# A recurrent layer on one core: hidden-state products of half B from bf16 parts, its two gates in one PSUM bank, x products without combinations

## The chip, the cores and the metric

The kernel runs on one NeuronCore of one Trainium2 chip. The metric is the device time of one execution in microseconds. A core has TensorE (PE, matrix products into PSUM), VectorE (DVE), ScalarE (ACT), GpSimd (POOL) and SyncE (SP, which issues DMAs here). They run at the same time, each its own instructions in order, and wait for each other through semaphores. In the profile's rows PEld is TensorE's weight load, the loading of the operand that stays in the array while the other one streams past it.

## The reference

A gated recurrent layer over 512 time steps, batch 8, 512 inputs, 512 hidden units; all float32. Cut to what matters:

```python
def step(h, x_t):
    fused = sigmoid(concat([x_t, h]) @ w_W + w_b)      # 1024 x 1024
    hidden_state, output_state = split(fused, 2)       # r and z
    memory_state = x_t @ wx_W + wx_b + hidden_state * (h @ wh_W + wh_b)
    h_new = output_state * h + (1.0 - output_state) * tanh(memory_state)
    return h_new, h_new
out = x + scan(step, h0, x)
```

Below, r and z are the two sigmoids and hh is `h @ wh_W + wh_b`. Each step needs the h of the step before, so the 512 steps follow one another; only the products with x can be done ahead.

## The kernel before, in words

**Layout.** The 512 hidden units are cut into four chunks k of 128, and the 128 partitions hold the units of a chunk in four strips of 32. A product takes a chunk of h (128 x 32: 8 batch columns for each of four steps of a group, so that the step's rows fall where its place in the group wants them; the other columns hold zeros) as the operand that stays, streams weights past it, and writes 32 PSUM partitions, one strip j. Four strips, four products side by side.

**Halves and banks.** The units are also cut into two halves: A (chunks 0 and 1) and B (chunks 2 and 3). Bank A (192 columns) gathers hh, z and r of half A, bank B (128 columns) r and hh of half B, bank C (64 columns) z of half B. A step runs its products in the order of `ORDER`: "A0 B0 A1 A2 A3 B1 B2 B3 C0 C1 C2 C3", letter and chunk of h. A0, B0 and A1 need only the new h of half A, A2 that of half B too. Behind them a step takes seven x products (`take(later, 7)`).

**The x side.** Four steps are a group; banks are kept twice, for even and odd groups. The x products of two groups are formed together with seven instead of eight half products (`products`), from sums of weights (`weight_sum`, DVE, in steps 1 to 8) and sums of x (`x_sum`, POOL), collected in the two banks `xps` and put together by DVE and ACT (the `o, u` branches). `spread` copies them into the banks A, B and C, `turn_x` turns the x part of the memory state into its place.

**A step after its products.** DVE turns r, hh and z of a half from PSUM to SBUF (32 x 32 block transposes), ACT takes the sigmoids (r into `md0`, 1-z into `hd0`). `memory` is a scan over (0, hh, r, x) tuples that gives r*hh+x for one chunk of 8 batch columns, then tanh on ACT; `update` is a scan that gives the new h of a chunk. DVE's order is: r, h, z and the two memories of half A, r and h of half B, first update of A, z of B, second update of A, memories and updates of B. POOL adds x and h into the output tile after the updates of B, first half B, then half A. `idle` memsets of one element on DVE stand behind the z transpose and at the step's end.

**Names.** `tr`, `tz`: turned gates; `md0`, `md1`, `hd0`: operands of the scans; `m`: memory state; `hTA`, `hTB`: the states, eight buffers each; `ot`: output tile; `xin`, `head`: x.

All engines' orders are the order of the code (`manual_schedule`). SP loads x in chunks of 16 steps and stores the output likewise; all weights are loaded once, at the start.

Of the kernel before, what the change touches and what calls it, by code (L numbers as in the profile page):

```python
# [7 lines left out]
F32 = mybir.dt.float32  # L8
# [13 lines left out]
DVE_FILL = 23  # L22
IDLE = 3
# [9 lines left out]
HALF = 192  # L33

AL, BE = (0, slice(64, 256)), (0, slice(256, 448))
GA, DE = (1, slice(64, 256)), (1, slice(256, 448))

XP = {"A": slice(0, 192), "X": slice(192, 320), "C": slice(320, 384), "B": slice(384, 512)}
# [3 lines left out]
def tile_cond_rnn_residual(  # L42
# [5 lines left out]
    wa_d: bass.AP,  # L48
    wb_d: bass.AP,
    wb3_d: bass.AP,  # L50
# [83 lines left out]
    def wh(bank, k, j):  # L134
        return wa[:, k, j] if bank == "A" else wb[:, k, j, {"C": slice(0, 64), "B": slice(64, 192)}[bank]]
# [3 lines left out]
    def pair(n, name, rows, slots):  # L139

        return const.tile([P, 2, rows, slots], F32, name=name).rearrange("p c n s -> p n c s")

    NH = 2 * GS
    hT = [[pair(n, f"hT{n}{i}", 32, 3) for i in range(NH)] for n in "AB"]

    md0 = [[pair(n, f"md0{n}{i}", 32, 2) for i in range(2)] for n in "AB"]
    md1 = [[pair(n, f"md1{n}{i}", 32, 2) for i in range(2)] for n in "AB"]
    hd0 = [[pair(n, f"hd0{n}{i}", B, 3) for i in range(2)] for n in "AB"]  # L150
# [7 lines left out]
    for j in range(NQ):  # L158
        nc.vector.memset(ones[32 * j : 32 * j + 1, j], 1.0)

    nc.scalar.activation(const.tile([P, 1], F32, name="table"), zeros[:, :1], AF.Sigmoid)
    for n, t_ in enumerate(hd0[0] + hd0[1] + md0[0] + md0[1] + hT[0] + hT[1]):
# [3 lines left out]
    idle = const.tile([P, IDLE], F32, name="idle")  # L166

    tw = [const.tile([P, 2, NQ, HALF], F32, name=f"tw{n}") for n in range(4)]
    sx = [[const.tile([P, 2, GS * B], F32, name=f"sx{n}{q}") for q in range(2)] for n in range(4)]
    step_bias = const.tile([P, HALF], F32, name="stepbias")  # L170
    even = const.tile([P, 256], F32, name="even")
    odd = [const.tile([P, 256], F32, name=f"odd{q}") for q in range(2)]
    both = const.tile([P, HALF], F32, name="both")

    def state(hf, i, slot=2):

        s = i % GS
        return hT[hf][i % NH][:, B * s : B * s + B, :, slot]

    ctx.enter_context(tc.manual_schedule())  # L180
    banks = [
        {n: psum.tile([P, w], F32, name=f"{n}{q}") for n, w in BANKS.items()}
        for q in range(2)
    ]
    xps = [psum.tile([P, 512], F32, name=f"xp{q}") for q in range(2)]
# [17 lines left out]
    nc.vector.tensor_copy(bias, xps[0])  # L203
    for hf in range(2):
        for slot in (0, 2):
            nc.vector.tensor_copy(
                state(hf, 0, slot), hin[:, 2 * hf : 2 * hf + 2].rearrange("p c b -> p b c")
            )
# [13 lines left out]
    def seed(g):  # L222

        nc.scalar.copy(xps[g % 2], bias)  # L224

    def prefill(g):

        c, t0 = divmod(g * GS, TC)
        for k in range(NQ):
            for j in range(NQ):  # L230
                mm(
                    xps[g % 2][32 * j : 32 * j + 32, 64:448],
                    x_of(c, k, t0, GS),
                    wx[:, k, j, :],
                )
            yield

    def late(g):

        if g == 0:  # L240
            return xps[0][:, 256:512]
        return even if g % 2 == 0 else odd[g // 2 % 2]

    def part(g, c0, c1):

        return late(g)[:, c0 - 256 : c1 - 256] if c0 >= 256 else xps[g % 2][:, c0:c1]

    def spread(g, names):

        for n in names:  # L250
            nc.scalar.copy(banks[g % 2][n], part(g, XP[n].start, XP[n].stop))

    def turn_x(g, e):

        c0 = XP["X"].start + 32 * e
        nc.vector.transpose(md1[e // 2][g % 2][:, :, e % 2, 1], part(g, c0, c0 + 32))

    def reg(r):
        return xps[r[0]][:, r[1]]

    def wx_of(kh, ch):
        return wx[:, 2 * kh : 2 * kh + 2, :, HALF * ch : HALF * ch + HALF]

    def x_half(o, n, kh):

        return x_of(o // 2, slice(2 * kh, 2 * kh + 2), 8 * (o % 2) + GS * n, GS)

    def weight_sum(n, k=slice(0, 2), j=None):

        a, b = [  # L270
            (wx_of(0, 1), wx_of(0, 0)),
            (wx_of(1, 1), tw[0]),
            (wx_of(1, 1), wx_of(0, 1)),
            (wx_of(1, 0), tw[1]),
        ][n]
        at = (slice(0, P), k, slice(0, NQ) if j is None else slice(2 * j, 2 * j + 2))
        nc.vector.tensor_tensor(tw[n][at], a[at], b[at], ALU.subtract)

    def x_sum(o, n):

        t_ = [q[o % 2] for q in sx]
        a, b, op = [
            (x_half(o, 1, 0), x_half(o, 1, 1), ALU.add),
            (t_[0], x_half(o, 0, 0), ALU.subtract),
            (x_half(o, 0, 0), x_half(o, 1, 0), ALU.subtract),
            (x_half(o, 0, 1), t_[1], ALU.subtract),
        ][n]
        nc.gpsimd.tensor_tensor(t_[n], a, b, op)

    def products(o):  # L290

        t_ = [q[o % 2] for q in sx]
        for to, lhs, rhs in (
            (AL, x_half(o, 0, 0), wx_of(0, 0)),
            (DE, t_[0], tw[0]),
            (BE, t_[1], tw[1]),
            (AL, x_half(o, 0, 1), wx_of(1, 0)),
            (GA, t_[2], tw[2]),
            (BE, t_[3], wx_of(1, 1)),
            (GA, x_half(o, 1, 1), tw[3]),  # L300
        ):
            for k in range(2):
                for j in range(NQ):
                    mm(reg(to)[32 * j : 32 * j + 32], lhs[:, k], rhs[:, k, j])
                    yield
# [7 lines left out]
    def x_side():  # L313
        for o in range(2, NG // 2):
            yield from products(o)

# [3 lines left out]
    later = x_side()  # L320
    first = {g: prefill(g) for g in (1, 2, 3)}
    weight_sum(0)
    weight_sum(2)
    spread(0, "BCA")
    for e in range(NQ):
        turn_x(0, e)

    pool_done = {}
    for i in range(T):
        g, s = divmod(i, GS)  # L330
        c, t = divmod(i, TC)
        ps = banks[g % 2]
# [5 lines left out]
        for n in (ORDER if i else FIRST).split():  # L338
            if n == "x":
                take(first[1], 1)  # L340
                continue
            bank, k = n[0], int(n[1])
            hs = hT[k // 2][i % NH][:, :, k % 2, 2]
            for j in range(NQ):
                j = (j + turn[0]) % NQ
                to = ps[bank] if i or bank != "A" else xps[0][:, XP["A"]]
                mm(to[32 * j : 32 * j + 32, :], hs, wh(bank, k, j))
        if i < 5:
# [87 lines left out]
        if i == 0:  # L436

            seed(2)
# [167 lines left out]
```

## Time and profile before

| what | value |
|---|---|
| time, median of 3 runs | 1670.06 us (1669.73 to 1671.35) |
| profiled execution, span | 1670.8 us |
| PE busy | 1659.0 us, 99% |
| DVE busy | 1090.5 us, 65% |
| ACT busy | 1029.9 us, 62% |
| POOL busy | 301.9 us, 18% |
| DMA, share of 16 engines | q1 4.0%, instructions 1.8% |
| granted TensorE clock, mean | 0.999 |

The profiled execution's own time is its span: the first to the last instruction. A row of a group shows line, engine, operation, what it writes `<-` what it reads, partitions x elements and type, how often, then its busy time in us, the mean ns of one, and the idle time of the engine before it with what ended that. A row of a timeline begins with start and length in us; neighbouring instructions of a kind are merged (`x16`), and the length is that of the whole group. The ends of matmuls are modelled and they are pipelined, so how fast products follow each other is read from start to start. Every matmul of the program is line 188, a helper's; the tile tells which it is.

### The profile page before, as it was taken

The page shows a single profiled execution, that of the slowest core. Times are in us where ns is not written, and L with a number is a line of the kernel's source. Part 1 is how long each engine was busy: PE and PEld are TensorE (multiplying, and loading weights), DVE is VectorE, ACT ScalarE, POOL GpSimd, SP SyncE. Part 2 cuts the span into 40 slices and gives each one's busy share as a digit, 9 for nine tenths or more (in the row PEclk, how much of TensorE's full clock was granted, in tenths as well). Part 3 has the DMA queues.
Part 4 walks back from the last instruction along what each step waited for, and adds up shares of the span by engine and source line. Part 5 has one row for each costly group of instructions (what it writes and reads, how often), then busy time and mean ns, then how long its engine had stood idle before and what let it go on. Part 6 is the DMA issues. An engine that isn't in the chain of part 4 may idle for free.

```text
span 1670.8 us, 129875 instructions
## 1 busy us (share of the span) xinstructions
PE 1659.0 (99%) x56238; PEld 1637.5 (98%) x56238; DVE 1090.5 (65%) x9387; ACT 1029.9 (62%) x5822; POOL 301.9 (18%) x1281
## 2 busy tenths in 40 slices
PE   8999999999999999999999999999999999999998
PEld 5999999999999999999999999999999999999997
DVE  6666666666666666666666666666666666666666
ACT  3666666666666666666666666666666666666665
POOL 1111111111111111111111111111111111111111
PEclk9999999999999999999999999999999999999999
DMA  4000000000000000000000000000000000000000
GB/s 179 17 5 17 18 18 17 17 6 17 17 18 18 5 17 18 17 17 5 18 17 17 18 11 12 18 17 17 18 5 17 17 18 17 5 17 12 11 12 10
DMA packets 11525, 31.40 MB, mean 19 GB/s; under 512 B 1220, under 2 KB 1732, under 8 KB 10824
## 3 DMA queue, kind: packets, MB, share of 16 engines
q1 hardware_dynamic: 10800, 22.94, 4.0%
q8 instruction: 440, 7.21, 1.8%
q14 instruction: 133, 1.09, 0.2%
q10 hardware_dynamic: 152, 0.16, 0.0%
HBM read 14.70 MB, written 8.39 MB: 14 GB/s over the span
## 4 chain that ended last, share of the span: by engine, by line
PE 98%; DVE 1%; DMA 0%; issue 0%; ACT 0%
PE A L188 44%; PE B L188 23%; PE xp L188 20%; PE C L188 12%; DMA rows<-in_bias_dram 0%; DVE tr L374 0%; DVE m L358 0%; DVE tz L374 0%; DVE md1B L390 0%; DVE md1A L390 0%; DVE hTA L358 0%; DVE bias L203 0%; ACT hTB L216 0%; ACT xp L224 0%; DVE rows L120 0%
## 5 line engine op out<-in xcount | busy, mean ns | idle before, releaser
L188 PE MATMUL A<-wa,hTA 128*32 128x192 f32 x8176 | 638.2, 329 | 2.3 <-DVE hTA L358 2.3
L188 PE MATMUL B<-wb,hTA 128*32 128x128 f32 x8192 | 573.8, 273 | 0.0
L188 PE MATMUL A<-wa,hTB 128*32 128x192 f32 x8176 | 507.4, 326 | 0.5 <-DVE hTB L358 0.5
L188 PEld LDWEIGHTS B<-wb,hTA 128*32 128x32 f32 x8192 | 471.2, 122 | 1.4 <-issue 0.2
L374 DVE STREAM_TRANSPOSE tr<-A 128x64 f32<-128x64 f32 x511 | 127.7, 250 | 463.5 <-PE A L188 463.5
L188 PE MATMUL B<-wb,hTB 128*32 128x128 f32 x8192 | 398.9, 273 | 0.0
L188 PEld LDWEIGHTS A<-wa,hTA 128*32 128x32 f32 x8176 | 385.4, 123 | 7.6 <-DVE hTA L358 4.0
L188 PEld LDWEIGHTS A<-wa,hTB 128*32 128x32 f32 x8176 | 372.9, 122 | 2.7 <-DVE hTB L358 0.8
L216 ACT ACTIVATE md0A<-tr 128x16 f32<-128x16 f32 x512 | 112.3, 219 | 421.0 <-DVE tr L374 421.0
L507 POOL TENSOR_TENSOR ot<-xin,hTB 128x16 f32<-128x16 f32 x503 | 125.9, 250 | 1324.5 <-DVE hTB L358 1314.0
L188 PEld LDWEIGHTS B<-wb,hTB 128*32 128x32 f32 x8192 | 321.5, 122 | 0.1
L188 PE MATMUL C<-wb,hTA 128*32 128x64 f32 x8192 | 289.4, 219 | 0.0
L188 PE MATMUL C<-wb,hTB 128*32 128x64 f32 x8192 | 288.9, 220 | 0.2 <-issue 0.2
L188 PEld LDWEIGHTS C<-wb,hTA 128*32 128x32 f32 x8192 | 266.7, 122 | 0.0
L188 PE MATMUL xp<-tw,sx 128*32 128x192 f32 x2976 | 237.2, 326 | 0.1
L188 PEld LDWEIGHTS C<-wb,hTB 128*32 128x32 f32 x8192 | 229.2, 123 | 0.4 <-issue 0.4
L358 DVE TENSOR_TENSOR_SCAN hTB<-hd0B,hTB 128x24 f32<-128x24 f32 x1024 | 157.8, 195 | 101.0 <-ACT hTB L216 99.8
L358 DVE TENSOR_TENSOR_SCAN hTA<-hd0A,hTA 128x24 f32<-128x24 f32 x1024 | 191.0, 187 | 0.0
L188 PE MATMUL xp<-wx,xin 128*32 128x192 f32 (+1 forms) x2048 | 182.4, 331 | 0.7 <-issue 0.5
L216 ACT ACTIVATE hd0B<-tz 128x16 f32<-128x16 f32 x512 | 115.2, 225 | 93.7 <-DVE tz L374 93.7
L216 ACT ACTIVATE hTB<-hTB 128x16 f32<-128x16 f32 x512 | 120.5, 235 | 79.8 <-DVE hTB L358 72.3
L216 ACT ACTIVATE hTB<-m 128x8 f32<-128x8 f32 x1024 | 160.6, 206 | 0.0
(92 smaller groups left out, 2489.6 us busy)
## 6 DMA issues: line engine op xcount, KB each, us to landing
xin<-in_x_dram SPq DMA_DIRECT2D x31, 256.0 KB, 3.5
out_dram<-ot SPq DMA_DIRECT2D x31, 256.0 KB, 2.2
wx<-in_wx_dram SPq DMA_DIRECT2D x4, 768.0 KB, 7.1
wa<-in_wa_dram SPq DMA_DIRECT2D x4, 384.0 KB, 8.9
wb<-in_wb_dram SPq DMA_DIRECT2D x1, 1152.0 KB
wb<-in_wb_dram SPq DMA_DIRECT2D x1, 384.0 KB, 11.1
out_dram<-ot SPq DMA_DIRECT2D x1, 192.0 KB, 3.9
head<-in_xh_dram ACTq DMA_DIRECT2D x1, 144.0 KB, 5.0
```

The source lines that it names most:

```text
L188: nc.tensor.matmul(out_, lhsT, rhs, start=start, stop=False, skip_group_check=True)
L216: inst = nc.scalar.activation(out_, in_, func, **kw).ins
L358: return nc.vector.tensor_tensor_scan(*[t_[:, :, c_].rearrange("p n c s -> p (n c s)") for t_ in (out_, d0, d1)], 0.0, ALU.mult, ALU.add,).ins
L374: inst = nc.vector.transpose(t_.rearrange("p c n -> p (c n)"), raw[n][hf]).ins
L507: return engine.tensor_tensor(ot[:, t, 2 * hf : 2 * hf + 2, :].rearrange("p c n -> p n c"), x_of(c, slice(2 * hf, 2 * hf + 2), t, 1).rearr ...
```

## The change

1. hh of half B no longer is in fp32 products of bank B. Its weights (`whole`) are split once, in step 0, into three bf16 parts (`ends` holds the first and the last, `middle` the second), by two ACT copies and two POOL subtracts. The state is split every step into three pieces, by two POOL subtracts for each half (`split`): each piece is the upper 16 bits of what is left, read in place as bf16 (`hi`). The pieces stand side by side as 24 columns. For each chunk and strip there are two bf16 products: the pieces against `ends` (128 columns) and against `middle` (64 columns), into a bank `hps` of their own. A row of the bank holds the bias; DVE turns the bank as a whole (128 columns), and the memory scan of half B adds the eight partial sums up, so that it has 9 elements for a batch column, 72 in all, instead of 2 and 16. In step 0 the product is fp32.
2. z and r of half B share bank B; bank C is gone. The order is "A0 A1 B0 A2 A3 B1 H0 H1 H2 H3 B2 B3", H being hh of half B. The operand that stays is cut to the columns up to the step's own (8, 16, 24 or 32).
3. x products are plain: `prefill`, one chunk of x a step, four products of 384 columns, two groups ahead. Weight sums, x sums and the putting together are gone; ACT seeds two halves of the bank with the bias instead.
4. DVE's order is: r, h, z and one memory scan (32 elements, with one tanh) of half A, turn of the hh bank, r of B, both updates of A, z of B, memories of B, every second step one turn of x (64 columns), updates of B. The idle memsets are gone. The copy of A's new state into its place for the next scan moves on ACT ahead of B's tanh. POOL's order is: split of A, add of A, split of B, add of B, each behind the updates of its half.
5. The weights of half B come in three transfers instead of two, hh first.

```diff
-ORDER = "A0 B0 A1 A2 A3 B1 B2 B3 C0 C1 C2 C3"
+ORDER = "A0 A1 B0 A2 A3 B1 H0 H1 H2 H3 B2 B3"
-FIRST = "A0 x A1 x A2 x A3 B0 B1 B2 B3 C0 C1 C2 C3"
+FIRST = "A0 x A1 x A2 x A3 x H0 H1 H2 H3 B0 B1 B2 B3"
-BANKS = {"A": 192, "B": 128, "C": 64}
+BANKS = {"A": 192, "B": 128}
+XC = slice(64, 448)
+ROWS = 48
+NES = (2, 9)
...
-    wb = const.tile([P, NQ, NQ, 192], F32, name="wb")
-    nc.sync.dma_start(out=wb[:, :3], in_=wb_d)
-    nc.sync.dma_start(out=wb[:, 3], in_=wb3_d)
+    whole = const.tile([P, NQ, NQ, 2, 32], F32, name="whole")
+    nc.sync.dma_start(out=whole, in_=wh_d)
+    wb = const.tile([P, NQ, NQ, 128], F32, name="wb")
+    for k in range(2):
+        nc.sync.dma_start(out=wb[:, 2 * k : 2 * k + 2], in_=wb_d[k])
...
+    def split(hf, i):
+        at = [slice(24 + B * n, 32 + B * n) for n in range(3)]
+        t_, h_ = hT[hf][i % NH], hi[hf][i % NH]
+        for n in range(2):
+            nc.gpsimd.tensor_tensor(
+                t_[:, :, at[n + 1], 2], t_[:, :, at[n], 2], h_[:, :, at[n], 2], ALU.subtract
+            )
+    def pieces(k, i):
+        return hi[k // 2][i % NH][:, k % 2, 24:, 2]
...
+    def split_weights():
+        nc.scalar.copy(ends[:, :, :, :, 0], whole)
+        nc.gpsimd.tensor_tensor(rest, whole, ends[:, :, :, :, 0], ALU.subtract)
+        nc.scalar.copy(middle, rest)
+        nc.gpsimd.tensor_tensor(ends[:, :, :, :, 1], rest, middle, ALU.subtract)
...
-            hs = hT[k // 2][i % NH][:, :, k % 2, 2]
+            if bank == "H" and i:
+                for q in range(2):
+                    for j in range(NQ):
+                        j = (j + turn[0]) % NQ
+                        to = hps[32 * j : 32 * j + 24]
+                        mm(*[(to, pieces(k, i), ends[:, k, j]), (to[:, :, 0], pieces(k, i), middle[:, k, j])][q],
+                           start=(k == 0 and q == 0))
+                continue
+            hs = hT[k // 2][i % NH][:, k % 2, 24 - B * s : 32, 2]
+            m = B * s + B
...
-        if i < 5:
-            take(first[(i + 3) // 2], 2)
-        else:
-            take(later, 7)
-            turn[0] += 7
+        if i and g + 2 < NG:
+            take(later[g + 2], 2 if i == 3 else 1)
...
-        turn_r(0)
-        turn_h(0)
-        turn_z(0)
-        memory(0, 0)
-        memory(0, 1)
-        turn_r(1)
-        turn_h(1)
-        update(0, 0)
-        turn_z(1)
-        tc.add_manual_dep(update(0, 1), r_done[1].name, SYNC)
+        gate_r(0, turned("r", 0))
+        nc.vector.transpose(
+            md1[0][g % 2][:, :, :, :, 0].rearrange("p s c b -> p c s b"), ps["A"][:, :HU]
+        )
+        gate_z(0, turned("z", 0))
+        memory(0, slice(0, 2))
+        nc.vector.transpose(
+            md1[1][g % 2][:, s].rearrange("p c b e -> p c e b")[:, :, :8], hps.rearrange("p c e n -> p (c e n)")
+        )
+        gate_r(1, turned("r", 1))
+        update(0, 0)
+        update(0, 1)
+        gate_z(1, turned("z", 1))
+        if i < T - 1:
+            nc.scalar.copy(state(0, i + 1, 0), state(0, i + 1))
+        memory(1, slice(0, 1))
+        memory(1, slice(1, 2))
         if i == 0:
-            seed(2)
+            split_weights()
...
-        memory(1, 0)
-        memory(1, 1)
+        if s % 2 == 0 and g + 1 < NG:
+            turn_x(g + 1, s // 2)
         update(1, 0)
         update(1, 1)
-        for hf in range(2):
-            act(("h", hf, (i + 1) % NH), state(hf, i + 1, 0), state(hf, i + 1), AF.Copy)
+        if i < T - 1:
+            nc.scalar.copy(state(1, i + 1, 0), state(1, i + 1))
...
-        for n in range(IDLE - 1):
-            nc.vector.memset(idle[:, n : n + 1], 0.0)
...
-        for hf in (1, 0):
-            pool_done[i + 1] = add(hf, nc.gpsimd)
+        split(0, i + 1)
+        add(0, nc.gpsimd)
+        split(1, i + 1)
+        pool_done[i + 1] = add(1, nc.gpsimd)
```

More of the change, by code (lines that the diff above doesn't have):

```diff
@@ L236, in prefill @@
             yield
[L238 to L305, printed above, removed]
+    def spread(g, n):
+        nc.scalar.copy(banks[g % 2][n], xps[g % 2][:, XP[n]])
@@ L319, in tile_cond_rnn_residual @@
     warm()
[L320 to L326, printed above, removed]
+    later = {g: prefill(g) for g in range(1, NG)}
+    spread(0, "A")
+    spread(0, "B")
+    for hf in range(2):
+        turn_x(0, hf)
     pool_done = {}
@@ L500, in tile_cond_rnn_residual @@
[L500 to L505 removed]
+            seed(2)
+        if s < 2 and g + 1 < NG:
+            spread(g + 1, "AB"[s])
+        elif s > 1 and g + 3 < NG:
+            c0 = XC.start + 192 * (s - 2)
+            seed(g + 3, slice(c0, c0 + 192))
```

237 lines of the change are left out of this document (91 added, 146 removed).

## The prediction

> **What bounds the kernel now.** I read the page first, then the tile view of the gate transposes, then the timeline of the last two steps, where no x products are left and the engines can be seen one at a time.
>
> ```profile
> span 1670.8 us, 129875 instructions
> PE 98%; DVE 1%; DMA 0%; issue 0%; ACT 0%
> L188 PE MATMUL B<-wb,hTA 128*32 128x128 f32 x8192 | 573.8, 273 | 0.0
> L374 DVE STREAM_TRANSPOSE tr<-A x511: 245/250/253, 22.6 to 1665.8; 128x64 f32<-128x64 f32 x171
> ```
>
> The chain is TensorE for 98% of the span. The transpose of half A's r gate runs once a step: 510 intervals from 22.6 to 1665.8 us, 3.222 us each; 27.6 us lie outside. B counts 8192 for 512 steps of two h chunks and four output strips, 4096 matmuls, so an fp32 matmul is two instructions. Now the ruler:
>
> ```profile
> 23.36 1.47 PE L188 MATMUL xp<-wx,xin 128*32 128x384 f32 x16
> 24.65 0.51 PE L188 MATMUL A<-wa,hTA 128*32 128x192 f32 x8
> ...
> 1664.02 0.19 PEld L188 LDWEIGHTS A<-wa,hTA 128*32 128x32 f32 x8 [0.39 <-DVE hTA L358]
> 1664.02 0.55 PE L188 MATMUL A<-wa,hTA 128*32 128x192 f32 x8 [0.24 <-DVE hTA L358]
> ...
> 1664.39 0.40 PE L188 MATMUL B<-wb,hTA 128*32 128x128 f32 x8
> ...
> 1664.56 0.31 DVE L358 TENSOR_TENSOR_SCAN hTB<-hd0B,hTB 128x24 f32<-128x24 f32 x2 [0.20 <-ACT hTB L216]
> ...
> 1664.82 0.58 PEld L188 LDWEIGHTS A<-wa,hTB 128*32 128x32 f32 x16
> ...
> 1664.93 0.83 PE L188 MATMUL A<-wa,hTB 128*32 128x192 f32 x16
> ...
> 1665.58 0.40 PE L188 MATMUL B<-wb,hTA 128*32 128x128 f32 x8
> ...
> 1665.80 0.62 PE L188 MATMUL B<-wb,hTB 128*32 128x128 f32 x16
> 1665.83 0.25 DVE L374 STREAM_TRANSPOSE tr<-A 128x64 f32<-128x64 f32 x1 [0.95 <-PE A L188]
> 1666.01 0.21 DVE L390 STREAM_TRANSPOSE md1A<-A 128x64 f32<-128x64 f32 x1
> 1666.12 0.22 ACT L216 ACTIVATE md0A<-tr 128x16 f32<-128x16 f32 x1 [0.98 <-DVE tr L374]
> ...
> 1666.24 0.41 PE L188 MATMUL C<-wb,hTA 128*32 128x64 f32 x16
> ...
> 1666.37 0.28 DVE L358 TENSOR_TENSOR_SCAN m<-md0A,md1A 128x16 f32<-128x16 f32 x2
> ...
> 1666.46 0.41 PE L188 MATMUL C<-wb,hTB 128*32 128x64 f32 x16
> ...
> 1666.59 0.31 ACT L216 ACTIVATE hTA<-m 128x8 f32<-128x8 f32 x2
> ...
> 1666.84 0.20 DVE L358 TENSOR_TENSOR_SCAN hTA<-hd0A,hTA 128x24 f32<-128x24 f32 x1
> 1666.96 0.22 DVE L374 STREAM_TRANSPOSE tz<-C 128x64 f32<-128x64 f32 x1
> ```
>
> Four strips run side by side, so 16 instructions are four rounds. From the start of one group to that of the next: two A chunks 0.65 us (1664.93 to 1665.58), one B chunk 0.22 (1665.58 to 1665.80), two C chunks 0.22 (1666.24 to 1666.46), two x chunks of 384 columns 1.29 (23.36 to 24.65). Before, a step needs 4 A (1.30), 4 B (0.87), 4 C (0.44) and 7 x matmuls of 192 columns, 3.5 rounds of 0.1625 (0.57): 3.18 of the 3.222 us. PE is the bound, with 0.04 us of waits. What lies just under it shows where no x is left:
>
> ```profile
> 1647.36 0.25 DVE tr L374
> ...
> 1650.44 0.25 DVE tr L374
> ```
>
> Here PE has 2.61 us of work and the period is still 3.08: the recurrence of half A, from A's last product through DVE and ACT to the next A0. So about 0.14 us is all that stands between the two.
>
> **PE's work.** Removed: C, 0.44 us, and 7 x matmuls, 0.57. Added: four x matmuls of 384 columns, 0.645, and for hh of half B 16 bf16 products of 128 columns and 16 of 64. [...]
>
> ```profile
> 2.52 0.31 PE L188 MATMUL B<-none 128*128 128x128 bf16 x1
> 2.63 0.26 PE L188 MATMUL C<-none 128*128 128x64 bf16 x1
> 2.70 3.38 PE L188 MATMUL xp<-zeros 128*128 128x512 f32 x4
> ```
>
> bf16: 0.11 us for 128 columns, 0.86 ns each. fp32, four instructions of 512 columns in 3.38 us: at most 1.65 ns a column. Hence a bf16 instruction is half an fp32 one: 128 columns cost what C's 64 cost, 0.055 us a round, 64 columns 0.028. Four rounds of each: 0.33 us. The fp32 product that follows came 0.07 us after a bf16 one, so changing type drains nothing. Sum: 1.30+0.87+0.645+0.33 = 3.15, only 0.03 under before.
>
> But each instruction has its own weight load. After the wait at 1664.02 the two A rounds took 0.37 us to 1664.39 instead of 0.325: a load that isn't hidden holds its round about 0.04 us. That is hidden under 0.055, not under 0.028. The new loads have 24 columns instead of 32:
>
> ```profile
> L188 PEld LDWEIGHTS xp<-zeros 128*128 128x128 f32 x2 | 0.3, 188 | 0.6 <-issue 0.6
> ...
> L188 PEld LDWEIGHTS xp<-wx,xin 128*32 128x32 f32 x1006 | 47.6, 110 | 0.9 <-issue 0.8
> ```
>
> (188-110)/96 = 0.8 ns a column, so 8 fewer save 6 ns. I take 0.037 us for the four middle rounds: +0.04 us. Bounds: 0 and 4 x 0.017 = 0.07. PE: 3.19 us, no gain at all. [...]
>
> **The new chain.** Before, half B's r and h were ready with C and x behind them. Now B2 and B3 come last, only 0.645 us of x follows, and in DVE's program order the two updates of half A stand behind B's r transpose, which waits for B3. Call M the start of B3's last instruction.
>
> - Half A: M's matmul lasts 0.27, and DVE starts 0.07 later (A's last product ended 1664.93+0.83 = 1665.76, its transpose began 1665.83; bound below 0.03, as 1001.07+0.33 to 1001.43 in the fence below). So B's r transpose is at M+0.34. The next DVE instruction follows 0.18 later (1665.83 to 1666.01): update of A. Update to released weight load 0.26 (1664.56 to 1664.82), load to product 0.04. A0 at M+0.82. From A0 to M: A0, A1 0.65, B0 0.22, A2, A3 0.65, B1 0.22, hh 0.37, B2 0.22, first half of B3 0.11, 0.02 for the strips' offset: 2.46. Loop 3.28.
> - Half B: transpose M+0.34; sigmoid 0.29 later (1665.83 to 1666.12); scan 0.25 (to 1666.37); tanh 0.22 (to 1666.59), with 72 elements instead of 16: 56 x 1.06 ns = 0.06 more; tanh to update 0.25 (to 1666.84); weight load 0.26; product 0.04; the copy of A's state, put between z's sigmoid and this tanh on ACT, takes 0.02 more than the scan lets show. A2 at M+1.73. PE's own work from M to A2 is 0.11+0.645+0.65+0.22 = 1.62, so A2 waits 0.11. From A2 to M 1.59. Loop 3.32 us.
>
> ```profile
> 1001.07 0.33 PE L188 MATMUL A<-wa,hTB 128*32 128x192 f32 x1
> ...
> 1001.43 0.25 DVE L374 STREAM_TRANSPOSE tr<-A 128x64 f32<-128x64 f32 x1 [0.94 <-PE A L188]
> ...
> L277 DVE TENSOR_TENSOR tw<-wx,tw 128x384 f32<-128x384 f32 x8 | 4.1, 518 | 0.0
> ...
> L475 DVE TENSOR_TENSOR odd<-xp,both 128x192 f32<-128x192 f32 x1 | 0.3, 316 | 0.0
> ```
>
> 1.06 ns an element is (518-316)/192 of these two rows. The scan of 72 is bounded by 0 and by twice that, +0.06. The removed idle memsets, weight sums and x sums cost nothing, and save nothing, off this chain. The transpose of the 128 hh columns starts about 0.1 before M and has until M+0.34; at two 64-column ones, 0.36, it is hidden. The same calculation for the tail of before gives 3.07 where 3.08 was measured (A0 to A's last product 1.38, then 0.39+0.29+0.25+0.22+0.25+0.26+0.04).
>
> **GpSimd's four new subtracts.** They start when the updates end, so while DVE scans. What meeting costs:
>
> ```profile
> 32.48 0.52 DVE L277 TENSOR_TENSOR tw<-wx,tw 128x384 f32<-128x384 f32 x1
> ...
> 32.53 0.58 POOL L507 TENSOR_TENSOR ot<-head,hTB 128x16 f32<-128x16 f32 x1 [3.13 <-DVE hTB L358]
> 33.07 0.24 POOL L507 TENSOR_TENSOR ot<-head,hTA 128x16 f32<-128x16 f32 x1
> ```
>
> An add of 0.24 us took 0.58 while DVE read two operands, and ended 0.11 after DVE: one waited for the other. Now the first subtract comes at M+0.87 (second update of A ends at M+0.79, 0.08 to GpSimd), B's first scan at M+0.88. The scan can lose 0 (it is first) to 0.24 (it waits for all of an add); the row has DVE first and unharmed, 0.52 as the mean of 518, so I stay near 0: +0.03. The pieces of half B are ready at about M+2.4 (last update M+1.8, two subtracts 0.24 each with their waits), the product that needs them is due at M+2.77: hidden by 0.37.
>
> PE meets that wait in order: behind it stand the rest of hh, B2, B3 and x, and so all of half B.
>
> **Beside it.** The same weight bytes come in three transfers instead of two on SP's queue, ahead of the same x load: they land before step 0 either way; seeds and spreads (0.3 us each) stay behind the last state copy on ACT, which then idles until the next r. At the start the weights are split, in a row and ahead of the hh of step 1:
>
> ```profile
> L503 POOL TENSOR_TENSOR stepbias<-bias 128x192 f32<-128x192 f32 x1 | 0.6, 587 | 0.0
> ...
> L224 ACT COPY xp<-bias 128x512 f32<-128x512 f32 x2 | 1.2, 585 | 0.0
> ```
>
> Two copies of 512 elements are 1.17 us, two subtracts, at (587-244)/176 = 1.95 ns an element over the 0.24 us of 16, 2.4 us; 1.1 of the 3.6 are hidden before hh is due, and the first state pieces come 1.2 later, 0.2 of it hidden: +3.5 us, once.
>
> **Sum.** 3.32+0.03 = 3.35 us a step; 27.6+510 x 3.35+3.5 = 1740 us, against the profile's 1670.8, which is 0.7 above the median of 1670.06.
>
> **Rivals.**
> 1. *PE stays the bound, faster.* The one mechanism: half B's loop is under the 1.62 us that PE covers, from 0.11 us less than my rows. For it: the lag of 0.03 instead of 0.07 was seen. Against: half A's loop, all from rows, is 3.28. At 3.15 to 3.19 us a step: 1638 to 1658.
> 2. *GpSimd holds a scan up*, every step, by a whole operation: 3.32+0.24 = 3.56, 1847 us. For it: the 0.58 us row; against: it shows DVE unharmed. [...]
> 3. *Pieces late*: two subtracts at 0.58 are 0.68 later than I have them, 0.31 beyond the cover: 3.63, 1883 us.
> 4. *bf16 rounds as slow as full weight loads* (0.110 each, 0.88 for hh instead of 0.37): 3.35+0.51 = 3.86, 2000 us; then the change doesn't do what it says. The hidden loads of C's 0.055 rounds are against it.
>
> **Chances.** Forecast 0.73 (3.24, with the lag at 0.03 and loads hidden and no meeting, to 3.49, with 0.07 of load and the scan losing up to 0.14); rival 1 0.11; 2 0.09; 3 0.04; 4 0.03. Range 1672 to 1825: on each side about half of the way from the forecast's own ends (1684, 1811) to the next rival. Below 0.2%, 3.3 us, nothing can be told from no change. Faster 0.11, same 0.03, slower 0.86.
>
> **What would show it.** Idle time of PE before A2 by a DVE update of half B, about 0.1 us a step, and before A0; B's r transpose waiting for PE B; hh rounds of 0.055 and 0.037; tanh of half B about 0.84 us after that transpose; GpSimd's subtracts at 0.25. Wrong if the transposes of A's r lie 3.2 us or less apart, or if PE waits for GpSimd.

## The result and the profile after

| | kernel before | changed kernel |
|---|---|---|
| time, median of 4 runs each | 1670.7 us (1669.73 to 1672.69) | 1772.93 us (1772.39 to 1774.46) |
| profiled execution, span | 1670.8 us | 1772.7 us |
| one step, median of the intervals between two transposes of half A's r | 3.21 us | 3.40 us |
| granted TensorE clock, mean | 0.999 | 0.997 |

The change costs 6.1 per cent: ratio 1.0609, 95% interval 1.0594 to 1.0624. The forecast was 1740 us; 33 us are missing from it.

First the page of the changed kernel, its span and the chain by engine; then the row of half A's r transposes from its tile view.

```profile
span 1772.7 us, 123454 instructions
...
PE 97%; DMA 1%; DVE 1%; POOL 0%; issue 0%; ACT 0%; SPq 0%; DVEq 0%
```

```profile
L345 DVE STREAM_TRANSPOSE tr<-A x511: 249/250/251, 24.6 to 1767.2; 128x64 f32<-128x64 f32 x171
```

The chain still names TensorE for 97%, and this misleads here: the ends of matmuls are modelled, and a wait of 0.2 us for a weight load falls under the modelled tail of the product before it. The waits of the weight loads (engine, operation, `<-` what was waited for: us in total, times, longest) tell it better:

```profile
PEld A L210 <- DVE hTA L335: 264.1, 510, 0.7
PEld A L210 <- DVE hTB L335: 137.2, 508, 0.3
```

In every step TensorE's load for an A product waits once for a VectorE update of half A and once for one of half B. The kernel before had about a dozen such waits in all. Most of one step in the timeline (start, length, instruction):

```profile
1001.76 0.24 PE L210 MATMUL hps<-ends,hTA 128*24 128x128 bf16 x4
...
1001.82 0.21 PE L210 MATMUL hps<-middle,hTA 128*24 128x64 bf16 x4
1001.84 0.24 PE L210 MATMUL hps<-ends,hTA 128*24 128x128 bf16 x4
...
1002.11 0.62 PE L210 MATMUL B<-wb,hTB 128*24 128x128 f32 x16
...
1002.47 0.39 DVE L386 STREAM_TRANSPOSE md1B<-hps 128x128 f32<-128x128 f32 x1
1002.54 0.83 PE L210 MATMUL xp<-wx,xin 128*32 128x384 f32 x8
...
1002.80 0.25 DVE L345 STREAM_TRANSPOSE tr<-B 128x64 f32<-128x64 f32 x1
...
1003.08 0.23 ACT L249 ACTIVATE md0B<-tr 128x16 f32<-128x16 f32 x1 [0.27 <-DVE tr L345]
...
1003.19 0.87 PE L210 MATMUL A<-wa,hTA 128*32 128x192 f32 x16
1003.35 0.31 DVE L335 TENSOR_TENSOR_SCAN ce(0, 1, None)_286_30274<-md0B,md1B 128x72 f32<-128x72 f32 x1
...
1003.69 0.22 ACT L249 ACTIVATE hTB<-ce(0, 1, None)_286_30274 128x8 f32<-128x8 f32 x1
...
1003.88 0.40 PE L210 MATMUL B<-wb,hTA 128*32 128x128 f32 x8
...
1003.94 0.40 DVE L335 TENSOR_TENSOR_SCAN hTB<-hd0B,hTB 128x24 f32<-128x24 f32 x2
1004.26 0.51 PEld L210 LDWEIGHTS A<-wa,hTB 128*32 128x32 f32 x16 [0.24 <-DVE hTB L335]
```

B0 starts at 1003.88 and takes 0.22, so TensorE is free for A2 at 1004.10; A2's load comes at 1004.26. The loop that sets the end is r transpose of half B, sigmoid, scan of 72, tanh, update, A2, and round again. Its pieces beside those of the prediction:

| piece of half B's loop | predicted, us | in this step, us |
|---|---|---|
| r transpose to sigmoid | 0.29 | 0.28 (1002.80 to 1003.08) |
| sigmoid to scan | 0.25 | 0.27 (to 1003.35) |
| scan to tanh | 0.30 | 0.34 (to 1003.69) |
| tanh to update | 0.25 | 0.25 (to 1003.94) |
| update to A2's load | 0.26, and 0.03 for GpSimd at the scan | 0.32 (to 1004.26) |
| load to product, A2 to the next r transpose | 0.04 + 1.59 + 0.34 = 1.97 | 1.94 (3.40 less the 1.46 above) |
| sum | 3.35 | 3.40 |

### The profile page after: what moved, and what is told of

It is laid out like the page before. It is cut to its first block, busy times and chain, and to the rows that moved or that the text cites. A ratio compares the mean times of both kernels' runs of the same rounds, so it can differ in the third digit from the quotient of the medians.

```text
span 1772.7 us, 123454 instructions
## 1 busy us (share of the span) xinstructions
PE 1752.0 (99%) x53262; PEld 1199.9 (68%) x53262; DVE 1284.5 (72%) x6955; ACT 1039.3 (59%) x5118; POOL 679.4 (38%) x3081
## 4 chain that ended last, share of the span: by engine, by line
PE 97%; DMA 1%; DVE 1%; POOL 0%; issue 0%; ACT 0%; SPq 0%; DVEq 0%
PE A L210 44%; PE B L210 25%; PE xp L210 18%; PE hps L210 10%; DMA wb<-in_wb_dram 1%; DMA wx<-in_wx_dram 0%; DVE tr L345 0%; DVE md1B L386 0%; POOL rest L238 0%; POOL ends L240 0%; DVE tz L345 0%; DVE hTA L335 0%; DVE md1A L381 0%; ACT middle L239 0%; ACT ends L237 0%
## 5 line engine op out<-in xcount | busy, mean ns | idle before, releaser
L193 POOL TENSOR_TENSOR hTA<-hTA 128x16 f32<-128x16 f32 x1022 | 261.2, 256 | 850.7 <-DVE tz L345 792.0
L210 PE MATMUL A<-wa,hTA 128*16 128x192 f32 x8176 | 439.0, 332 | 3.8 <-DVE hTA L335 3.7
L210 PE MATMUL A<-wa,hTB 128*16 128x192 f32 x8176 | 438.8, 332 | 2.3
L210 PE MATMUL xp<-wx,xin 128*32 128x384 f32 x4032 | 417.6, 487 | 0.0
L210 PEld LDWEIGHTS A<-wa,hTA 128*16 128x16 f32 x8176 | 209.1, 108 | 300.7 <-DVE hTA L335 264.1
L210 PE MATMUL B<-wb,hTA 128*8 128x128 f32 (+3 forms) x8192 | 412.3, 273 | 0.0
L210 PEld LDWEIGHTS A<-wa,hTB 128*16 128x16 f32 x8176 | 209.8, 108 | 172.6 <-DVE hTB L335 137.2
L210 PE MATMUL B<-wb,hTB 128*8 128x128 f32 (+3 forms) x8192 | 320.1, 274 | 2.0 <-DMA wb<-in_wb_dram 2.0
L210 PEld LDWEIGHTS B<-wb,hTA 128*8 128x8 f32 (+3 forms) x8192 | 258.6, 106 | 74.9 <-issue 0.5
L193 POOL TENSOR_TENSOR hTB<-hTB 128x16 f32<-128x16 f32 x1022 | 226.1, 221 | 214.7 <-DVE hTB L335 174.4
```

The lines of the kernel that those rows point to most:

```text
L193: nc.gpsimd.tensor_tensor(t_[:, :, at[n + 1], 2], t_[:, :, at[n], 2], h_[:, :, at[n], 2], ALU.subtract)
L210: nc.tensor.matmul(out_, lhsT, rhs, start=start, stop=False, skip_group_check=True)
```

## The experiments

The theory after the result: this loop sets the time, its scan of 72 elements costs about 2 ns an element and its first update is stretched by GpSimd. Rivals: TensorE's own work, with the plain x products, is the bound after all; the pieces come late.

**Half of the x products left out** (e1)

```diff
-                    xps[g % 2][32 * j : 32 * j + 32, XC],
+                    xps[g % 2][32 * j : 32 * j + 32, XC][:, : 384 if g < 2 else 192],
...
-                    wx[:, k, j, :],
+                    wx[:, k, j, : 384 if g < 2 else 192],
```

> From group 2 on the plain x products stream 192 of their 384 columns (half of the x terms is left out); all else is as in the changed kernel. Theory: a step is bound by the loop of half B (last B product, transpose of r, sigmoid, scan of 72, tanh, update, product A2), in which no x product stands: TensorE's x chunk falls from 0.645 to about 0.33 us, A0 waits that much longer for half A's update, the step stays 3.40 us, time 1773 +- 6 us. Rival 'TensorE's own work, with the eighth x product, is the bound': 0.32 us less in each of some 508 steps, about 1610 us.

1770.57 us, a ratio of 1.0533 (1.0508 to 1.0558) to the kernel before on that chip. In its timeline the A product starts 0.64 us after x, although half as many columns stream, and its load waits:

```profile
1001.69 0.51 PE L210 MATMUL xp<-wx,xin 128*32 128x192 f32 x8
1002.33 0.84 PE L210 MATMUL A<-wa,hTA 128*8 128x192 f32 x16
```

```profile
1002.33 0.45 PEld L210 LDWEIGHTS A<-wa,hTA 128*8 128x8 f32 x16 [0.51 <-DVE hTA L335]
```

So 0.32 us of TensorE's work in every step, 163 us in all, is worth 1 to 2 us: TensorE isn't the bound, and the eighth x product is paid for by nobody here. It shows too that half A's update is ready just as the full x chunk ends (0.64 against 0.65): the loop of half A lies close under that of half B.

**GpSimd's adds last** (e2)

```diff
         split(0, i + 1)
-        add(0, nc.gpsimd)
         split(1, i + 1)
+        add(0, nc.gpsimd)
         pool_done[i + 1] = add(1, nc.gpsimd)
```

> GpSimd does both halves' piece subtractions first and both output adds after them, so that no add starts beside half B's first update. Theory: update(1,0) is stretched from 0.208 to 0.265 us by GpSimd's add that starts with it, on the loop that sets the step: back to 0.208, 0.057 us x 510 = 29 us less, about 1744 us; if the adds then meet another scan of a loop part of it is lost, up to 1760. Rival 'the stretch is the update's own cost as a scan of stride 3 rows, GpSimd has no part in it': row unchanged at 0.265, time 1773. Rival 'pieces come late': the adds out of their way would make the products of half B's pieces earlier, but these wait for nothing in the trace, so no gain by that.

1743.05 us, ratio 1.0369 (1.0348 to 1.0390): 29 to 30 us less than the changed kernel, as expected. The timeline of the changed kernel around the first update of half B (VectorE, then GpSimd):

```profile
1003.94 0.26 DVE L335 TENSOR_TENSOR_SCAN hTB<-hd0B,hTB 128x24 f32<-128x24 f32 x1
```

```profile
1003.92 0.23 POOL L424 TENSOR_TENSOR ot<-xin,hTA 128x16 f32<-128x16 f32 x1
```

The groups of half B's updates, count, busy time and mean ns of one, in the changed kernel and with the adds last:

```profile
L335 DVE TENSOR_TENSOR_SCAN hTB<-hd0B,hTB 128x24 f32<-128x24 f32 x1024 | 207.8, 238 | 23.1 <-ACT hTB L249 0.6
```

```profile
L335 DVE TENSOR_TENSOR_SCAN hTB<-hd0B,hTB 128x24 f32<-128x24 f32 x1024 | 207.7, 208 | 22.8 <-ACT hTB L249 0.6
```

The mean of 1024 falls by 30 ns, and one of two updates of a step is met: 60 ns a step. The add starts 0.02 us ahead of the update and holds it for 0.06, a quarter of its own length.

**A shorter scan** (e3)

```diff
-NES = (2, 9)
+NES = (2, 5)
...
-            md1[1][g % 2][:, s].rearrange("p c b e -> p c e b")[:, :, :8], hps.rearrange("p c e n -> p (c e n)")
+            md1[1][g % 2][:, s].rearrange("p c b e -> p c e b")[:, :, :4], hps[:, 0].rearrange("p c n -> p (c n)")
```

(with `hps` and `ends` laid out so that the first two parts' sums are 64 neighbouring columns)

> Only the partial sums with the first two parts of the weights (40 elements instead of 72 in half B's scan) are turned and added; the third part's products still run on TensorE but are left out of the sum. The transpose of the partial sums is 64 columns instead of 128. Theory: the scan costs 2.0 ns per element ((281-170 ns)/(72-16)), so it shortens by 32 x 2.0 = 0.063 us on the loop that sets the step: 0.063 x 510 = 32 us less, about 1740 us; the shorter transpose (0.39 to 0.25 us) frees VectorE just ahead of the transpose of r, at most 0.01 more. Rival 'the scan is 1.06 ns per element and its 281 ns come from GpSimd': 17 us less. Rival 'TensorE bound': no change, 1773.

1746.31 us, ratio 1.0388 (1.0367 to 1.0408): 26 to 27 us less where 32 were expected and 17 by the other price. The two scans of a step:

```profile
1000.48 0.24 DVE L335 TENSOR_TENSOR_SCAN ce(0, 1, None)_290_30696<-md0B,md1B 128x40 f32<-128x40 f32 x1
1000.64 0.21 DVE L335 TENSOR_TENSOR_SCAN ce(1, 2, None)_290_30699<-md0B,md1B 128x40 f32<-128x40 f32 x1
```

0.31 becomes 0.24 for 32 elements fewer: about 2.1 ns each. The prediction took 1.06 from an addition of two tensors. The step falls by 0.05 us (median 3.35), less than the scan's 0.066: by the medians the tanh now follows the scan's end by 47 ns instead of 34, and half B's first update, which GpSimd's add still meets, takes 284 ns instead of 269.

**hh last** (e4)

```diff
-ORDER = "A0 A1 B0 A2 A3 B1 H0 H1 H2 H3 B2 B3"
+ORDER = "A0 A1 B0 A2 A3 B1 B2 B3 H0 H1 H2 H3"
```

(and the transpose of `hps` behind half A's updates and half B's z)

> The hh rounds H0-H3 run after B2, B3 instead of ahead of them, and VectorE turns the partial sums after half A's updates and the z transpose of half B. Theory: the last product of B, which the loop of half B waits for, ends 0.35 us earlier; the scan then waits for the partial sums' transpose (end of the last H + 0.07 + 0.39, and the scan may begin some 0.07 before it is written out), about 0.2 us earlier against the end of TensorE's recurrent work than now: the wait of A2 (0.20 us) nearly goes, the step is 3.20 to 3.26 us, time 1667 to 1700, best guess 1680. Rival 'TensorE's own work already binds': 1773. Rival 'VectorE gets too full between transpose and scan': 1720 to 1773.

1920.97 us, ratio 1.1427 (1.1404 to 1.1450): a miss by 240 us, in the wrong direction. The timeline shows why:

```profile
1002.13 0.23 DVE L345 STREAM_TRANSPOSE tr<-B 128x64 f32<-128x64 f32 x1
1002.51 0.31 DVE L335 TENSOR_TENSOR_SCAN hTA<-hd0A,hTA 128x24 f32<-128x24 f32 x2 [0.15 <-ACT hTA L249]
...
1002.88 0.38 DVE L390 STREAM_TRANSPOSE md1B<-hps 128x128 f32<-128x128 f32 x1
1003.36 0.31 DVE L335 TENSOR_TENSOR_SCAN ce(0, 1, None)_264_27971<-md0B,md1B 128x72 f32<-128x72 f32 x1
```

The r transpose did come early. But the turn of the partial sums stood in VectorE's queue behind updates that waited for half A's tanh, and the scan that reads what it wrote began 0.10 us after its end; what had been hidden ahead of r now lay between r and the scan, 1.23 us from transpose to scan instead of 0.55. The 0.07 by which the expectation let the scan begin early was wrong: I had taken the delay to the next, independent instruction for that to one that uses the result.

**hh in fp32 again** (e5)

```diff
-            if bank == "H" and i:
...
+                    if i:
+                        hs, m = hT[k // 2][i % NH][:, k % 2, 24:32, 2], B
-                    mm(hps[32 * j : 32 * j + m, :, 0], hs, whole[:, k, j])
+                    mm(hps[32 * j : 32 * j + m, :, 0], hs, whole[:, k, j], start=(i > 0 and k == 0))
```

> The bf16 part alone is undone: hh of half B runs as four fp32 products of 64 columns (0.11 us each by the two 64-column chunks of the kernel before, 0.22 us), 0.44 us instead of 0.35 in every step; GpSimd's four subtractions a step and the split of the weights go, the sums of half B keep their nine slots. Theory: +0.09 on the way from A2 to the last B product, which lies on the loop that sets the step, -0.057 if the first update of half B is no longer met by a GpSimd operation: step 3.43 to 3.50 us, time 1788 to 1823. Rival 'the splitting costs more than the bf16 products save': below 1770.

1803.30 us, ratio 1.0657 (1.0616 to 1.0698), 30 to 31 us more than the changed kernel. The steps are 0.08 us longer; the split of the weights at the start, gone here, gives some 7 us back. The 0.08 are made of three parts: 0.09 more for hh, 0.06 less because half B's first update is no longer met (0.21 us), and some 0.045 more because GpSimd's add of half A now starts 0.03 us ahead of half B's first scan, which takes 0.35 us instead of 0.31. hh takes 0.44 us in TensorE (1001.50 to 1001.94), in the changed kernel 0.35 (1001.76 to 1002.11 above):

```profile
1001.50 0.41 PE L210 MATMUL hps<-whole,hTA 128*8 128x64 f32 x16
...
1001.94 0.62 PE L210 MATMUL B<-wb,hTB 128*24 128x128 f32 x16
```

So the bf16 products themselves do what they say. They need a scan of 72 elements, and 56 elements at 2.1 ns are 0.12 us on the same loop, more than the 0.09 that they save. (fp32 products with a short scan were not run.)

**The kernel before with an eighth product** (e6)

```diff
+        for n in range(8):
+            j = n % NQ
+            mm(reg(GA)[32 * j : 32 * j + 32], zeros[:, :32], tw[3][:, 0, j])
+            yield
...
-            take(later, 7)
-            turn[0] += 7
+            take(later, 8)
+            turn[0] += 8
```

> The kernel before with eight more x products of 192 columns per two groups (stationary operand zeros, so the sums stay), one a step: eight instead of seven, as many columns as the plain products have. Theory of the prediction: the kernel before is bound by TensorE's own work; 192 columns on one lane are 0.645/8 = 0.081 us, some 496 steps: +40 us over the before of the same chip. Rival 'before is bound by a loop through VectorE, and TensorE has room': no change.

1719.58 us against 1689.70 for the kernel before on that chip: ratio 1.0175 (1.0123 to 1.0226), 30 us and not 40. The median step rises from 3.21 to 3.27 us. The kernel before is bound by TensorE, as the prediction had it, but the added product costs 0.06 us and not 0.08; that seven products leave one of four strips short, which the eighth fills, would explain it and wasn't tried.

**Two parts of the weights** (e7)

```diff
-NES = (2, 9)
+NES = (2, 5)
...
-        nc.gpsimd.tensor_tensor(ends[:, :, :, :, 1], rest, middle, ALU.subtract)
...
-                        mm(*[(to, pieces(k, i), ends[:, k, j]), (to[:, :, 0], pieces(k, i), middle[:, k, j])][q],
+                        mm(*[(to[:, 0], pieces(k, i), ends[:, k, j, 0]), (to[:, 0], pieces(k, i), middle[:, k, j])][q],
```

(with the layout of the shorter scan, and GpSimd's adds last)

> The changed kernel with weights in two bf16 parts instead of three (the third part is left out of the products and of the sums), so half B's scan adds 40 elements, the hh rounds stream 64 columns each, the transpose of the partial sums is 64 wide; GpSimd's adds come after both halves' subtractions. Theory: -0.063 (scan), -0.057 (update no longer stretched), and with eight rounds of 0.028 us instead of four of 0.057 and four of 0.028, -0.12 between A2 and the last B product: step 3.40 - 0.24 = 3.16 us, time about 1650 (1640 to 1665), under the kernel before on the same chip. TensorE's own work would be 3.05 us. Rival 'the hh rounds of 64 columns don't get shorter because their loads show': 1710.

1675.71 us, ratio 0.9907 (0.9875 to 0.9938): under the kernel before on that chip (1689.70), though not under the 1670.7 of the first comparison, and 26 us above the guess. Its median step, 3.207 us, is as long as that of the kernel before, 3.211. Beside the 3.16 us expected, the 0.05 are in the hh rounds, which the timeline shows from the first to the B product behind them:

```profile
1002.76 0.21 PE L210 MATMUL hps<-ends,hTA 128*24 128x64 bf16 x4
1002.79 0.21 PE L210 MATMUL hps<-middle,hTA 128*24 128x64 bf16 x4
...
1003.04 0.30 PE L210 MATMUL B<-wb,hTB 128*8 128x128 f32 x4
```

Eight rounds take 0.28 us, 0.035 each. In the changed kernel a round of 128 and one of 64 columns took 0.09 together (0.35 for four such pairs), 0.03 for the shorter one beside 0.055 for the longer. That fits loads that hide under a longer round ahead of them and show where every round is short; the loads alone were not varied.

**Two parts, hh last, turn right behind r** (e8)

```diff
+        gate_r(1, turned("r", 1))
         nc.vector.transpose(
             md1[1][g % 2][:, s].rearrange("p c b e -> p c e b")[:, :, :4], hps[:, 0].rearrange("p c n -> p (c n)")
         )
-        gate_r(1, turned("r", 1))
         update(0, 0)
-        update(0, 1)
         gate_z(1, turned("z", 1))
+        update(0, 1)
```

> As e7, with the hh rounds after B2 and B3, and the turn of the partial sums right behind the transpose of r, ahead of half A's updates, so that it doesn't queue behind their wait for the tanh as in e4. Theory: r's transpose starts 0.22 us earlier against the end of TensorE's recurrent work, the partial sums' turn is ready about when the sigmoid is: step 3.08 to 3.13 us, near TensorE's own work of 3.05; time 1605 to 1640. Rival 'VectorE's queue again': the scan waits for the turn or half A's update is held by it, 1650 or more.

1650.45 us, ratio 0.9751 (0.9713 to 0.9789), the fastest of all, though above the guessed 1605 to 1640. The step is 3.16 us. TensorE is nearly full: 3.05 by the prediction's ruler, 0.06 in the hh rounds as just shown, 0.04 for a wait of A0. In the timeline the r transpose now follows half A's scan without a wait for TensorE, and the turn stands behind it; then come half A's tanh, its first update and the load of A0 that waits for it:

```profile
1001.14 0.22 DVE L344 STREAM_TRANSPOSE tr<-B 128x64 f32<-128x64 f32 x1
...
1001.25 0.22 ACT L248 ACTIVATE hTA<-ce(0, 2, None)_308_32567 128x16 f32<-128x16 f32 x1
...
1001.43 0.30 DVE L386 STREAM_TRANSPOSE md1B<-hps 128x64 f32<-128x64 f32 x1
1001.60 0.17 DVE L334 TENSOR_TENSOR_SCAN hTA<-hd0A,hTA 128x24 f32<-128x24 f32 x1
...
1001.82 0.47 PEld L210 LDWEIGHTS A<-wa,hTA 128*16 128x16 f32 x16 [0.50 <-DVE hTA L334]
```

The rival "VectorE's queue again" named 1650 or more, and the time lies there. Part of it is seen: the update comes 0.35 us after its tanh has begun, where 0.25 is usual, because the turn stands ahead of it, and A0's wait of 0.04 would fit into that delay. The scan of half B waits in the queue too (0.78 us from the r transpose by the median, instead of 0.55), but A2 no longer waits for it: the loop of half B isn't the bound any more.

**The start** (e9 and e10)

The changed kernel's steps 0 and 1 in the timeline, and then three stretches of the window view (length, busy time and count of PE, PEld, DVE, ACT and POOL, granted clock, DMA share, GB/s):

```profile
20.28 0.63 PE L210 MATMUL B<-wb,hTB 128*8 128x128 f32 x16 [2.03 <-DMA wb<-in_wb_dram]
...
23.36 2.13 POOL L238 TENSOR_TENSOR rest<-whole,ends 128x1024 f32<-128x1024 f32 x1 [19.52 <-ACT ends L237]
...
26.64 2.12 POOL L240 TENSOR_TENSOR ends<-rest,middle 128x1024 bf16<-128x1024 f32 x1 [1.16 <-ACT middle L239]
...
27.56 1.28 DVE L335 TENSOR_TENSOR_SCAN 0slice(0, 2, None)_1_403<-md0A,md1A 128x32 f32<-128x32 f32 x1 [2.44 <-ACT md0A L249]
...
29.29 0.31 PE L210 MATMUL hps<-ends,hTA 128*24 128x128 bf16 x4 [4.54 <-POOL hTA L193]
```

```profile
21.00:25.00 4.00, 3.39 (x48) 1.74 (x48) 1.89 (x12) 1.91 (x6) 1.64 (x1) 0.58 0.04 13
...
29.30:33.00 3.70, 3.56 (x64) 1.95 (x68) 1.85 (x9) 0.96 (x5) 1.39 (x7) 0.50 0.00 0
33.00:37.00 4.00, 4.00 (x108) 2.74 (x104) 1.72 (x10) 1.41 (x7) 0.83 (x4) 0.80 0.02 4
```

From half A's r transpose of step 1 to that of step 2 pass 10.65 us instead of 3.40. The weights of a split are 1024 elements, not the 512 of the prediction; TensorE idles for 4.5 us and then runs at a granted clock of 0.50 up to 33 us. The clock was low once before, 0.58 from 21 to 25 us, behind the 2.03 us in which half B's products waited for their weights. That doesn't follow every time: in the second profile of the changed kernel (e11 below) the wait was 2.1 us and the clock stayed at 1.00 in those 4 us.

```diff
-            if bank == "H" and i:
+            if bank == "H" and i > 1:
...
-                    mm(hps[32 * j : 32 * j + m, :, 0], hs, whole[:, k, j])
+                    mm(hps[32 * j : 32 * j + m, :, 0], hs, whole[:, k, j], start=(i == 1 and k == 0))
```

> The changed kernel with hh of step 1 also as four fp32 products, so that TensorE first reads the bf16 weights in step 2. Theory: the 10.65 us between the r transposes of steps 1 and 2 hold a wait of 4.54 us for the split of the weights and a stretch in which TensorE then runs at about half its rate; both go, but GpSimd's subtractions of 2.1 us still hold half A's scan of step 1 (1.28 us instead of 0.23): 4 to 7 us less, 1766 to 1769 us; the interval falls to 4 to 6.5 us. Rival 'the wait only moves into step 2': the second interval rises by what the first loses, time as the changed kernel's on this chip within 1.5 us.

1768.88 us, ratio 1.0483 (1.0458 to 1.0507), beside 1771.82 for the changed kernel on the same chip: 3 us, under the 4 to 7 expected. The interval falls to 7.96 us, not to 4 to 6.5; the next one is 3.39 as before, so the wait did not move into step 2. TensorE no longer waits for the pieces, but its x products wait for ACT's copy of the bias, half A's sigmoid of step 1 stands on ACT behind the cast and three copies, and its scan is held by GpSimd just the same. The stretch at a lower clock didn't go either: 0.62 from 25 to 29 us.

```profile
24.21 1.04 ACT L239 CAST middle<-rest 128x1024 bf16<-128x1024 f32 x1 [2.25 <-POOL rest L238]
...
25.91 1.51 PE L210 MATMUL xp<-wx,xin 128*32 128x384 f32 x8 [2.34 <-ACT xp L257]
26.01 0.21 ACT L249 ACTIVATE md0A<-tr 128x16 f32<-128x16 f32 x1
...
26.25 1.28 DVE L335 TENSOR_TENSOR_SCAN 0slice(0, 2, None)_1_387<-md0A,md1A 128x32 f32<-128x32 f32 x1 [3.20 <-ACT md0A L249]
```

The same edit on the two-part kernel:

> Weights in two bf16 parts (the third part is left out), hh rounds last, partial sums turned right behind r, GpSimd's adds last, and hh of step 1 in fp32: the first interval, 7.9 us with the bf16 products in step 1, falls to 4 to 5.5 us, 2.5 to 4 us less than the run without it, 1646 to 1648 us where that ran at 1650; faster than the kernel before on the same chip by 1.3 to 2.6 per cent. Rival: the wait moves into step 2, 1650.

1650.56 us, ratio 0.9783 (0.9767 to 0.9799): nothing to be seen in the time, taken on another chip than the 1650.45. The first interval falls to 5.87 us, above the 4 to 5.5 expected; the first two intervals of its trace are 2.4 us shorter together, but its first step began 2.6 us later (22.0 and 24.6 us for the first of half A's transposes). Half B's first products wait 2.1 us for their weights in this trace and 0.6 in the other. Undecided.

**The two kernels once more** (e11 and e12)

> The changed kernel as it is, once more beside the kernel before, to see how far the two move from chip to chip: the kernel before was 1670.7, 1680.5 and 1689.7 us in the three comparisons so far. If before's extra time on those chips is its own, the changed kernel stays within 1770 to 1776 us here; if the chip slows both alike, both rise by the same share.

The changed kernel took 1771.82 us (1771.02 to 1774.07) where the kernel before took 1687.11: ratio 1.0502 (1.0485 to 1.0520). So the kernel before moves by up to 19 us from comparison to comparison and the changed one by one.

> The kernel before as it is. Its median was 1670.7 to 1689.7 us from comparison to comparison, the changed kernel's 1772.9 and 1771.8. Theory: the kernel before is bound by TensorE's own work, so every gap in which TensorE waits for nothing but its next instruction ('issue' in the waits: 8.0 + 1.1 us in some 30 gaps in the first profile, 17 to 19 us in the run with the eighth product) adds to its time, and the number of gaps differs from run to run; the changed kernel has 0.24 us a step of waits that take such a gap up. If this run is slower than 1675, its median step stays at 3.21 us and single steps of 3.4 to 4.0 us make up the rest, with correspondingly more 'issue'. Rival: the whole chip is slower, and the median step rises to 3.23 to 3.25 us.

1685.41 us, ratio to itself 1.0001 (0.9983 to 1.0018). The largest waits of TensorE's loads for nothing but their own issue between 40 and 1640 us, in the first profile of the kernel before:

```profile
PEld xp L188 <- issue: 1.9, 4, 0.7
...
PEld C L188 <- issue: 0.4, 1, 0.4
```

and in this one:

```profile
PEld xp L188 <- issue: 4.6, 13, 0.8
PEld C L188 <- issue: 3.8, 11, 0.7
PEld A L188 <- issue: 0.9, 4, 0.3
```

All such waits sum to 2.6 us there in the first profile and to 9.6 in this one; the start and the end hold another 7.0 and 5.7. The 29 steps of this profile in which they stand are 10.2 us longer in sum than as many median steps. The median step is 3.219 us against 3.211; but 45 steps from the fifth on are over 3.3 us long, against 10, and lie 13.1 us above 3.21 in sum against 3.0: 10 of the 12 us between the two spans, 7 of them in these waits. What lengthens the long steps without one (17 of the 45) isn't shown. The rival, a slower chip throughout, named a median step of 3.23 to 3.25.

## Why the prediction was right, and 33 us short

- *The bound moves from TensorE to half B's loop*: right. A2 waits as the prediction said, 0.16 us against 0.11; A0's wait, for which the prediction's rows leave 0.07 (M+0.82 against 0.755 of work), is near zero, since half A's update is ready just as x ends. Half of x left out changed nothing.
- *TensorE's work*: the hh rounds take 0.35 us, not 0.37. The 0.04 for loads that don't hide was too high here, where rounds of 64 and of 128 columns alternate. Without them the prediction's sum is 0.33; 0.35 lies halfway. The price of a bf16 column, half of that of an fp32 one, held (0.055 us for a round of 128, where an fp32 one takes 0.11). In the prediction's rows from the start of the kernel before a column of either takes about twice as long, 0.86 and at most 1.65 ns, at a granted clock of 1.00 from 1.5 to 7 us; why isn't shown. In rounds of 64 alone (weights in two parts) a round took 0.035 against 0.028. As TensorE isn't the bound, neither weighs in the changed kernel's time.
- *The scan of 72*: the largest mis-sized term. "56 x 1.06 ns = 0.06 more", with twice that as the bound; it costs 2.1 ns an element by the run with 40, the bound itself. In the loop that is 0.34 from scan to tanh against 0.30, since the 0.02 laid there for the copy of A's state didn't come. An element of the scan costs twice the 1.06 ns of one of the addition by which I had priced it; why isn't shown.
- *GpSimd*: right in kind, wrong in place and size. The +0.03 was laid at the first scan of half B; that one seems to be let through, 0.31 us beside 0.28 for the second (the first and second scan of half A in the kernel before, with no GpSimd instruction beside them, differ as much: 192 and 169 ns), and GpSimd's subtract is the one that gets longer (0.29 against 0.22). The price is 0.06 at the first update, where an add has a start of 0.02 us; 29 us when it was moved.
- *Pieces of half B hidden, hh's transpose hidden*: right. No steady row waits for GpSimd's pieces; the transpose ended just as r's began (1002.47 and 1002.80), so its cover was all but used up, as the run with hh last showed when it was gone.
- *The start*: "+3.5 us, once" was 7.25 (10.65 less a step of 3.40), since twice the elements are split, half A's scan is held, and TensorE runs at a lower granted clock behind its 4.5 us of idle time (0.50 from 29.30 to 33 us); how much each takes was not separated. "They land before step 0 either way" was wrong in this profile: half B's first products waited 2.03 us for their weights (2.1 in its second profile, 0.6 in that of the run on half of x). All before the first of half A's transposes and behind the last is 30.0 us here, 27.6 before.
- *In sum*: 0.0525 us in 510 steps, 26.8 us; 3.75 for the split; 2.4 for the rest of the start and the end. That is the 33 us.
- *Rivals*: TensorE as the bound fell with the run on half of x, pieces late and slow bf16 rounds by the trace. GpSimd holding a scan for a whole operation (1847 us) was off by a factor of four in the steps, 0.06 for 0.24. At the start it is seen: 1.28 us instead of 0.23 for half A's scan, which ended 0.08 us after GpSimd's subtract (27.56 + 1.28 and 26.64 + 2.12). In the steps the update lost only a quarter of the add's length, 0.06 of 0.23 us; what makes the two differ isn't shown.

What the change bought and paid for: TensorE's own work stayed nearly what it was, since plain x products cost in columns what hh in bf16 saves, while the loop of half B got a longer scan, a met update and its r products at the very end. With the weights in two parts, the adds moved and hh last the time, 1650 us, falls under the 1670 to 1690 of the kernel before, there at the price of the weights' third part; no version with all three parts did. Three parts in that last order, hh last and turned right behind r, were not run.

## What to carry to other kernels

When a change takes work off the engine that is the bound, work out the loop that comes next before counting the gain, piece by piece from a stretch of the trace where it already stands alone; here that loop was 0.14 us below. Price an operation by a row of the same operation: two sizes of it give the cost of an element. When an instruction is moved in a queue, ask what it will stand behind: a transpose that was free ahead of a wait cost 0.3 us a step behind it.

## What was not expected of the hardware

- The kernel before, bound by TensorE, takes gaps in TensorE's own issue at full price: steps with 9.6 us of them were 10.2 us longer in sum. Its two profiles hold 2.6 and 9.6 us of them between 40 and 1640 us, and its time moved from 1670 to 1690 us between comparisons. The changed kernel moved by 1 us; from 45 us on neither of its two profiles names such a wait. Whether its waits for VectorE take the gaps up or they don't arise isn't shown.
- An update of 24 elements that starts 0.02 us after a GpSimd addition takes 0.26 us instead of 0.21; a scan of 72 that starts 0.03 us after one takes 0.35 instead of 0.31; a scan of 32 that starts 0.9 us into a GpSimd subtraction of 1024 elements takes 1.28 instead of 0.23.
- After 4.5 us without products TensorE's granted clock was 0.50 in the mean of 3.7 us, and 0.80 in the 4 us behind them; waits of 2.0 and 2.1 us were followed by 0.58 in one profile and by 1.00 in another.
